# Attention beside feed-forward on one core: norm factors tied to the newest logit, the first tile's end in triple steps, list work held back and spread

## The chip, the cores and the metric

The kernel runs on one core of a Trainium2 chip. Its time is the device time of that core in microseconds (us). Before the change three runs took 1851.42, 1851.66 and 1855.57 us, median 1851.66. The profiled execution spans 1847.4 us.

The engines are named as the profile names them: PE is TensorE (PEld its weight loads), DVE is VectorE, ACT is ScalarE, POOL is GpSimd, SP is SyncE. A letter q behind the name stands for the engine's sequencer, which issues transfers.

## The reference

One graph layer on 4096 nodes with 512 features, then a residual and a norm. Only the part that matters:

```python
hs = layer_norm(x); ht = layer_norm(h_target)          # 4096 x 512 each
q = (ht @ Wq + bq).reshape(T, 8, 64) / 8
k = (hs @ Wk + bk).reshape(S, 8, 64);  v = (hs @ Wv + bv).reshape(S, 8, 64)
logits = jnp.where(adj != 0, einsum('thd,shd->hts', q, k), -1e30)
ctx = einsum('hts,shd->thd', softmax(logits), v)
ht = layer_norm(ht + ctx @ Wo + bo)
y = ht + gelu(ht @ W1) @ W2                            # 512 -> 2048 -> 512
return layernorm(x + y)
```

The adjacency matrix is symmetric and sparse: an edge is drawn with probability 0.00195 per ordered pair, then joined with its mirror image and the diagonal, which makes some 17 neighbours to a node, differing from node to node.

## The kernel before

The kernel works on neighbour lists. It has these streams of work, which one program of Python generators weaves together:

- *Projections*: `x` is normed and projected to keys and values, 32 blocks of 128 rows, and stored to a table `kvd` in HBM (one row per node, 1024 numbers).
- *Lists*: each of 32 tiles of 128 adjacency rows is loaded in four quarters of 512 KB; ScalarE takes their sign, VectorE picks the indices of the edges. Nodes are then sorted by degree in two parts of 16 tiles, and a record per node (degree, norm factors of its target row, neighbour indices) is scattered to HBM. Part one is done before the attention starts, part two beside it.
- *Front* of a target tile: its records say which 128 rows of `h_target` to gather; they are normed (line 990), transposed and multiplied with `Wq` to queries `tq`.
- *Attention*: for up to three neighbour slots at a time the K/V rows are gathered (128 rows of 4 KB a slot), multiplied with the query (line 1209), summed to logits `lg` (1213), exponentiated (1217, 1226), multiplied with the values (1173, 1193) and summed on TensorE (1181).
- *End* of a tile (`finish`): sums, reciprocals, the product with `Wo`, the second norm, and a transpose to `h2T`, which is the input of the feed-forward.
- *Feed-forward* of a group of one or two tiles: `pf` (1316), Gelu (1319), `po` (1325), last norm, scatter to `out`.

A generator's `yield cost` says how long its piece is reckoned to take; the stream with the least total goes next, and `yield None` sleeps until another stream has moved. The instructions are written down in this order, but each engine's program is then arranged at build by the framework from its own reckoning of what is ready when, within the dependencies. So a dependency that is added also moves an instruction in its engine's program.

The parts that the change touches (cuts marked with `# ...`):

```python
def quarter(i, h):                          # load a quarter of adjacency tile i
    if i < NA + FILL:                       # NA = 16, FILL = 5: the first 21 tiles
        a = ring[:, (i * NQ + h) % DEEP, :].bitcast(I32)
    else:
        a = turn_of("wide", wide)           # two buffers in turn
    nc.sync.dma_start(a, adj[i * P:(i + 1) * P, h * QW:(h + 1) * QW])
    return a

def edges(i):
    # ...
    for h in range(NQ):
        n = i * NQ + h
        while len(adjs) < min(n + 2, NT * NQ):
            adjs.append(quarter(*divmod(len(adjs), NQ)))
        a, adjs[n] = adjs[n], None
        sg = turn_of("signs", signs)
        nc.scalar.activation(sg, a, AF.Sign, accum_out=dpart[:, i, h:h + 1])      # L728
        ahead = min(n + DEEP - 1, n + 3 + n // 2)
        while len(adjs) < min(max(n + 3, min(ahead, (NA + FILL) * NQ)), NT * NQ):
            adjs.append(quarter(*divmod(len(adjs), NQ)))
        # ... VectorE: product with positions (L733), maxima of segments (L735)
        yield 2.0
    # ... VectorE: decode, sort, keep the rest of the list (L742 to L759)
    yield 4.0

def source(n, j):                           # keys and values of one block
    # ...
    for half, w in enumerate((wk, wv)):
        # ... four matmuls into pkv
        nc.scalar.copy(kvr[:, half * D:(half + 1) * D], pkv)                       # L931
    r0 = 1 + (g * G + j) * P
    nc.scalar.dma_start(kvd[r0:r0 + P, :], kvr)
    return 7.8

def front(i, idle=0):
    rec = recs[i]
    tq = sp.tile([P, 2 * D], F32, name="tq", bufs=3)
    t = tq[:, :D]
    gather(t, h_target, rec[:, TGT:TGT + 1])
    for _ in range(1 + idle):
        yield
    m = rec[:, RST:RST + 2].bitcast(F32)
    nc.scalar.activation(t, t, AF.Identity, bias=m[:, 1:2], scale=m[:, 0:1])       # L990
    yield
    # ... four transposes (L994), four scalings on ScalarE (L997), two yields,
    # ... four matmuls with Wq (L1003), three yields
    nc.vector.scalar_tensor_tensor(tq[:, :D], pq, HD ** -0.5, bqr, ...)            # L1008
    tqs[i] = tq

def first_fronts():                         # EARLY = 2
    for i in range(EARLY):
        prefetch(i)
    for i in range(EARLY):
        fronts[i] = front(i)
    while fronts:
        go_on()                             # one step of every front
        yield 4.0

def attention():
    tails, pend = [], []                    # tails: the ends of tiles under way
    def advance():
        go_on()
        for t in list(tails):
            if next(t, StopIteration) is StopIteration:
                tails.remove(t)
    # ... per tile, per set of up to three slots:
            lg = sp.tile([P, S, H], F32, name="lg")
            nc.vector.tensor_reduce(lg[:, :n, :], ...)                             # L1213
            # ... exp; advance(); yield; values of the set before; advance(); yield

def weights():                              # the last two quarters of W1 and W2
    for q, pool in enumerate(pools):
        yield 10.0
        load_quarter(pool, q + 2, nc.scalar)

def other_lists():                          # tiles 21 to 31, then the sort of part two
    for cost in ed:
        yield 1.5 * cost
    yield from sort(1)

_weave((projections(), 0), (prepare(), 0), (fill(), 0))
# ...
_weave((att, 0), (chain(feed(g) for g in range(len(GROUPS))), 0), (other_lists(), WAIT),
       (weights(), 0))                      # WAIT = 40
```

`prepare` makes the lists of part one, sorts it and runs `first_fronts`; `fill` makes the lists of five more tiles.

Of the kernel before, what the change touches and what calls it, by code (L numbers as in the profile page):

```python
# [8 lines left out]
F32 = mybir.dt.float32  # L9
# [434 lines left out]
def adj_resnorm_kernel(  # L444
# [88 lines left out]
    with tc.tile_pool(name="keep", bufs=1) as keep:  # L533
# [17 lines left out]
        with ExitStack() as late:  # L551
# [149 lines left out]
            held, moms = [], list(range(NT))  # L701
            mvh = wp.tile([P, NT, 2], F32, name="mvh")

            adjs = []
            DEEP = 8
            FILL = 5

            def quarter(i, h):
                if i < NA + FILL:
                    a = ring[:, (i * NQ + h) % DEEP, :].bitcast(I32)  # L710
                else:
                    a = turn_of("wide", wide)
                nc.sync.dma_start(a, adj[i * P:(i + 1) * P, h * QW:(h + 1) * QW])
                return a

# [47 lines left out]
            def keep_rest():  # L763

                while held:
                    nc.sync.dma_start(*held.pop())
# [97 lines left out]
            def project(order, t=None):  # L864
# [54 lines left out]
                def source(n, j):  # L919
                    g, hT = order[n], state[n][1]  # L920
                    if asked or moms:
                        kvr = sp.tile([P, 2 * D], F32, name="tq", bufs=3)
                    else:

                        kvr = ring[:, 8 + (n * G + j) % 3, :]
                    for half, w in enumerate((wk, wv)):
                        pkv = psi.tile([P, D], F32, name="pq", bufs=3)
                        for kc in range(KC):
                            nc.tensor.matmul(pkv, hT[:, kc, j * P:(j + 1) * P], w[:, kc, :],  # L929
                                             start=kc == 0, stop=kc == KC - 1)  # L930
                        nc.scalar.copy(kvr[:, half * D:(half + 1) * D], pkv)  # L931
                    r0 = 1 + (g * G + j) * P
                    nc.scalar.dma_start(kvd[r0:r0 + P, :], kvr)
                    return 7.8
# [23 lines left out]
                        yield cost  # L958


            recs, tqs, h2Ts, done, ready = {}, {}, {}, set(), []

            def gather(dst, table, idx):
                nc.gpsimd.indirect_dma_start(  # L964
# [21 lines left out]
                gather(t, h_target, rec[:, TGT:TGT + 1])  # L986
                for _ in range(1 + idle):
                    yield
                m = rec[:, RST:RST + 2].bitcast(F32)
                nc.scalar.activation(t, t, AF.Identity, bias=m[:, 1:2], scale=m[:, 0:1])  # L990
                yield
                pt = ps.tile([P, KC, P], F32, name="t", bufs=2)
                for kc in range(KC):
                    nc.tensor.transpose(pt[:, kc, :], t[:, kc * P:(kc + 1) * P], ident)  # L994
                hT = tq[:, D:].rearrange("p (c t) -> p c t", c=KC)
                for kc in range(KC):
                    nc.scalar.activation(hT[:, kc, :], pt[:, kc, :], AF.Identity,  # L997
                                         bias=b1r[:, kc:kc + 1], scale=s1c[:, kc:kc + 1])
                yield
                yield  # L1000
                pq = ps.tile([P, D], F32, name="t", bufs=2)
                for kc in range(KC):
                    nc.tensor.matmul(pq, hT[:, kc, :], wq[:, kc, :], start=kc == 0,  # L1003
                                     stop=kc == KC - 1)
# [141 lines left out]
            def first_fronts():  # L1146

                for i in range(EARLY):
                    prefetch(i)
                for i in range(EARLY):  # L1150
                    fronts[i] = front(i)
                while fronts:
                    go_on()
                    yield 4.0

            def attention():


                tails, pend = [], []

                def advance():
                    go_on()
                    for t in list(tails):
                        if next(t, StopIteration) is StopIteration:
                            tails.remove(t)

                def values(i, j0, n, kv, p, cps, after):

# [29 lines left out]
                for group in GROUPS:  # L1198
# [3 lines left out]
                    for i in group:  # L1202
                        cps = ps.tile([P, KC, P], F32, name="cps", bufs=2)
                        while k < len(SG) and SG[k][0] == i:
                            _, j0, n = SG[k]
                            while i not in tqs:
# [3 lines left out]
                                                    tq[:, :D].unsqueeze(1).to_broadcast([P, n, D]),  # L1210
                                                    ALU.mult)
                            lg = sp.tile([P, S, H], F32, name="lg")
                            nc.vector.tensor_reduce(lg[:, :n, :],  # L1213
                                                    kv[:, :n, :D].rearrange("p j (h d) -> p j h d", h=H),
                                                    AX.X, ALU.add)
# [223 lines left out]
            _weave((att, 0), (chain(feed(g) for g in range(len(GROUPS))), 0), (other_lists(), WAIT),  # L1439
# [36 lines left out]
```

## Time and profile before

| | before |
|---|---|
| time, median of 3 | 1851.66 us |
| span of the profile | 1847.4 us |
| mean granted TensorE clock | 0.964 |
| first multiply of a query with keys (L1209) | 311.25 us |
| first feed-forward matmul (L1316) | 369.81 us |
| last list quarter signed (L728) | 575 us |
| data moved | 463.27 MB |

Until some 290 us the projections and lists run, until about 1705 us attention and feed-forward together, and from there feed-forward alone. The profile's page gives, for each engine, its busy time and the busy share in 40 equal slices. A line of a group or of an order of time reads: line of the kernel, engine, operation, output from inputs, shapes, count; in brackets or behind a bar is the idle time of that engine just before, and what ended it. A wait reads: who waited, for whom, total us, how often, longest.

### The profile page before, as it was taken

The page shows a single profiled execution, that of the slowest core. Times are in us where ns is not written, and L with a number is a line of the kernel's source. Part 1 is how long each engine was busy: PE and PEld are TensorE (multiplying, and loading weights), DVE is VectorE, ACT ScalarE, POOL GpSimd, SP SyncE. Part 2 cuts the span into 40 slices and gives each one's busy share as a digit, 9 for nine tenths or more (in the row PEclk, how much of TensorE's full clock was granted, in tenths as well). Part 3 has the DMA queues.
Part 4 walks back from the last instruction along what each step waited for, and adds up shares of the span by engine and source line. Part 5 has one row for each costly group of instructions (what it writes and reads, how often), then busy time and mean ns, then how long its engine had stood idle before and what let it go on. Part 6 is the DMA issues. An engine that isn't in the chain of part 4 may idle for free. (4 is left out here: it accounts for less than half of the span.)

```text
span 1847.4 us, 22879 instructions
## 1 busy us (share of the span) xinstructions
PE 1693.9 (92%) x7030; PEld 1101.0 (60%) x7030; DVE 1428.8 (77%) x2596; ACT 1222.2 (66%) x3121; POOL 971.7 (53%) x834
## 2 busy tenths in 40 slices
PE   7999884697988989999998998999999999999997
PEld 3444332475655656767676656666666666666664
DVE  6999855999989838686968989979787797988200
ACT  5777634587877646686767867687767676787311
POOL 1000153856546577656567787776574665664001
PEclk9999987898999989999999999999999999999999
DMA  9999949988876738677769878687676767775000
GB/s 350 374 388 374 348 156 350 348 300 303 285 271 209 243 96 313 230 252 260 275 225 315 293 265 295 221 298 253 233 265 216 251 225 247 236 248 170 12 12 25
DMA packets 144396, 463.27 MB, mean 251 GB/s; under 512 B 20628, under 2 KB 25800, under 8 KB 144264
## 3 DMA queue, kind: packets, MB, share of 16 engines
q0 software_dynamic: 96656, 342.64, 54.2%
q1 hardware_dynamic: 39792, 96.00, 14.5%
q10 hardware_dynamic: 7816, 23.08, 3.3%
q8 instruction: 58, 0.95, 0.2%
q14 instruction: 74, 0.61, 0.1%
HBM read 430.76 MB, written 30.89 MB: 250 GB/s over the span
## 5 line engine op out<-in xcount | busy, mean ns | idle before, releaser
L964 POOL DMA_INDIRECT kv<-kvd,rec x603 | 744.9, 1235 | 395.1 <-PE cps L1181 157.2
L1325 PE MATMUL po<-w,gt 128*128 128x512 f32 x1024 | 470.4, 603 | 9.7 <-ACT gt L1319 7.2
L1316 PE MATMUL pf<-h2T,w 128*128 128x256 f32 (+1 forms) x2176 | 466.6, 368 | 1.1 <-issue 0.7
L1316 PEld LDWEIGHTS pf<-h2T,w 128*128 128x128 f32 x2176 | 388.7, 191 | 66.6 <-issue 22.4
L1209 DVE TENSOR_TENSOR kv<-kv,tq 128x1536 f32<-128x1536 f32 (+2 forms) x211 | 352.0, 1676 | 82.4 <-DMA kv<-kvd,rec 71.2
L1193 ACT ACTIVATE kv<-kv,pa 128x64 f32<-128x64 f32 x1520 | 390.8, 336 | 4.1
L1213 DVE TENSOR_REDUCE lg<-kv 128x24 f32<-128x1536 f32 (+2 forms) x211 | 350.2, 1667 | 1.1 <-DVE kv L1209 0.2
L1325 PEld LDWEIGHTS po<-w,gt 128*128 128x128 f32 x1024 | 190.7, 194 | 210.3 <-issue 201.5
L1181 PE MATMUL cps<-ident,kv 128*128 128x128 f32 x2008 | 264.6, 280 | 51.1 <-DMA kv<-kvd,rec 24.2
L1181 PEld LDWEIGHTS cps<-ident,kv 128*128 128x128 f32 x2008 | 238.2, 145 | 120.2 <-DVE kv L1173 51.5
L1173 DVE TENSOR_TENSOR kv<-kv,p 128x1024 f32<-128x1024 f32 (+1 forms) x211 | 251.5, 1194 | 41.2 <-ACT p L1217 28.8
L687 POOL TENSOR_TENSOR n_rs<-n_ve,mhalf 128x2 f32<-128x2 f32 (+2 forms) x51 | 47.7, 936 | 340.8 <-DVE n_ve L680 139.8
L728 ACT ACTIVATE kv<-kv 128x1024 uint8<-128x1024 int32 x128 | 134.7, 1054 | 76.8 <-DMA kv<-in_adj_dram 40.6
L1319 ACT ACT_TABLE_LOAD x104 | 133.4, 1283 | 1.6
L735 DVE MAX8 cand<-kv 128x8 uint16<-128x103 uint16 (+1 forms) x640 | 130.2, 252 | 1.7 <-issue 0.7
L1003 PE MATMUL t<-wq,tq 128*128 128x512 f32 x256 | 119.9, 611 | 12.1 <-ACT tq L997 12.1
L1319 ACT ACTIVATE gt<-pf 128x512 f32<-128x512 f32 x128 | 76.4, 597 | 81.0 <-PE pf L1316 66.7
L929 PE MATMUL pq<-wk,h2T 128*128 128x512 f32 x256 | 121.6, 618 | 5.2 <-ACT tq L931 3.7
L929 PE MATMUL pq<-wv,h2T 128*128 128x512 f32 x256 | 118.5, 606 | 6.7 <-ACT kv L931 5.5
L1107 PE MATMUL t<-wo,rb 128*128 128x512 f32 x256 | 120.7, 614 | 0.0
L990 ACT ACTIVATE tq<-tq,rec 128x512 f32<-128x512 f32 x32 | 26.0, 813 | 142.8 <-DMA tq<-in_L_gnn_h_target_dram,rec 136.3
L1217 ACT ACTIVATE p<-lg 128x24 f32<-128x24 f32 (+2 forms) x179 | 38.9, 218 | 94.6 <-DVE lg L1213 69.3
(156 smaller groups left out, 1603.3 us busy)
## 6 DMA issues: line engine op xcount, KB each, us to landing
kv<-in_adj_dram SPq DMA_DIRECT2D x128, 512.0 KB
kvd<-tq ACTq DMA_DIRECT2D x24, 512.0 KB
kv<-kvd,rec POOLq DMA_INDIRECT x603
kv<-in_L_gnn_h_target_dram SPq DMA_DIRECT2D x32, 256.0 KB
kv<-in_x_dram SPq DMA_DIRECT2D x15, 512.0 KB
rest_d<-gid SPq DMA_DIRECT2D x32, 160.0 KB
w<-in_L_gnn_W_dram SPq DMA_DIRECT2D x4, 1024.0 KB
kvd<-kv ACTq DMA_DIRECT2D x8, 512.0 KB
```

Source lines behind the costliest of these rows:

```text
L728: nc.scalar.activation(sg, a, AF.Sign, accum_out=dpart[:, i, h:h + 1])
L735: nc.vector.max(cand[:, h * SQ + s, :], wd[:, w0:w1])
L929: nc.tensor.matmul(pkv, hT[:, kc, j * P:(j + 1) * P], w[:, kc, :], start=kc == 0, stop=kc == KC - 1)
L964: nc.gpsimd.indirect_dma_start(out=dst, out_offset=None, in_=table[:, :], in_offset=bass.IndirectOffsetOnAxis(ap=idx, axis=0))
L1173: nc.vector.tensor_tensor(v4, v4, p[:, j0:j0 + m, :].unsqueeze(3) .to_broadcast([P, m, H, HD]), ALU.mult)
L1181: nc.tensor.matmul(cps[:, c, :], kv[:, j, D + c * P:D + (c + 1) * P], ident, is_transpose=True, start=j0 + j == 0 and c == 0, stop=j0 + n ...
L1193: nc.scalar.mul(v, v, pa[:, hd:hd + 1])
L1209: nc.vector.tensor_tensor(kv[:, :n, :D], kv[:, :n, :D], tq[:, :D].unsqueeze(1).to_broadcast([P, n, D]), ALU.mult)
L1213: nc.vector.tensor_reduce(lg[:, :n, :], kv[:, :n, :D].rearrange("p j (h d) -> p j h d", h=H), AX.X, ALU.add)
L1316: nc.tensor.matmul(pf[:, k, :], w1[(f0 + k) // KC][:, kc, (f0 + k) % KC * P:((f0 + k) % KC + 1) * P], h2T[:, kc, :w], start=kc == 0, stop= ...
L1319: nc.scalar.activation(gt, pf, AF.Gelu_apprx_tanh)
L1325: nc.tensor.matmul(po[j], gt[:, k, j * P:(j + 1) * P], w2[(f0 + k) // KC][:, (f0 + k) % KC, :], start=False, stop=f0 + k == FC - 1, skip_g ...
```

## The change

Four edits, all about order:

1. *Norm factors tied to the newest logit.* Ahead of a front's norm, VectorE writes the two norm factors over themselves with an operation that also reads the newest logit (`max(m, m)` with the logit as an ignored operand). So the norm can't be placed ahead of that logit. For the first two tiles the operand is a late K/V block of the projections (from the fifteenth pair on), their gathers are asked for at once, and the rest waits until such a block has been written down.
2. *First tile's end in triple steps.* Until the first `h2T` exists, each `advance` takes three steps of a tile's end in place of one.
3. *Lists held.* Once the first fronts are done, the next two quarters of adjacency get a one-column write of the newest logit ahead of their load, so that the load can't be placed ahead of the logits.
4. *Lists spread more widely.* A piece of list work beside the attention is reckoned at 1.8 of its cost in place of 1.5, and `keep_rest` stores what is left before the sort.

The purpose: engines should not stand at a transfer that is not there yet, the first gathers should have the transfer engines to themselves, and the first feed-forward should begin sooner.

```diff
-            adjs = []
+            adjs, held_back = [], []
@@ def quarter
                     a = turn_of("wide", wide)
+                    if fronts_done and len(held_back) < 2:
+                        held_back.append(i)
+                        nc.scalar.copy(a.bitcast(F32)[:, 0:1], latest[-1])
@@ def source
                         nc.scalar.copy(kvr[:, half * D:(half + 1) * D], pkv)
+                    if n >= 14:
+                        latest[:] = [kvr[:, 0:1]]
@@ def front
                 m = rec[:, RST:RST + 2].bitcast(F32)
+                nc.vector.scalar_tensor_tensor(m, m, latest[-1], m, op0=ALU.bypass, op1=ALU.max)
                 nc.scalar.activation(t, t, AF.Identity, bias=m[:, 1:2], scale=m[:, 0:1])
@@ def first_fronts
                     fronts[i] = front(i)
+                    step(fronts, i)
+                while not latest:
+                    yield None
@@ def attention
-                        if next(t, StopIteration) is StopIteration:
-                            tails.remove(t)
+                        for _ in range(1 if h2Ts or begun else 3):
+                            if next(t, StopIteration) is StopIteration:
+                                tails.remove(t)
+                                break
+                    if h2Ts:
+                        begun.add(True)
@@
                             lg = sp.tile([P, S, H], F32, name="lg")
+                            latest[:] = [lg[:, 0, 0:1]]
@@ ahead of the second weave
+            fronts_done.append(True)
             def other_lists():
                 for cost in ed:
-                    yield 1.5 * cost
+                    yield 1.8 * cost
+                keep_rest()
                 yield from sort(1)
```

More of the change, by code (lines that the diff above doesn't have):

```diff
@@ L958, in project @@
                         yield cost
-            recs, tqs, h2Ts, done, ready = {}, {}, {}, set(), []
+            recs, tqs, h2Ts, done, ready, latest = {}, {}, {}, set(), [], []
+            fronts_done = []
             def gather(dst, table, idx):
@@ L1156, in attention @@
             def attention():
-                tails, pend = [], []
+                tails, pend, begun = [], [], set()
                 def advance():
```

## The prediction

> **What bounds the kernel now.** I read the busy times and the slices first. TensorE is the fullest engine, and the slices say where it is not full.
>
> The page of the kernel before, busy times and three rows of its 40 slices (one slice is 46 us):
> ```profile
> PE 1693.9 (92%) x7030; PEld 1101.0 (60%) x7030; DVE 1428.8 (77%) x2596; ACT 1222.2 (66%) x3121; POOL 971.7 (53%) x834
> ...
> PE   7999884697988989999998998999999999999997
> ...
> DVE  6999855999989838686968989979787797988200
> ...
> PEclk9999987898999989999999999999999999999999
> ```
> TensorE lacks 153 us of the span, mostly early. From slice 38 on, VectorE is nearly done and TensorE still runs dense: the end is feed-forward work alone. So the time is TensorE's work plus its holes, and a hole closed anywhere moves the end. Busy time by stage gives TensorE's idle time: 0-262 us 25; 262-275 6; 275-311 16; 311-345 18; 345-370 9; 370-445 11; 445-690 23; 690-1705 33; the rest 5.
>
> Then TensorE's order of time at the change of stage (start, duration, last the idle time before it and what ended it):
> ```profile
> 264.94 3.70 PE L929 MATMUL pq<-wk,h2T 128*128 128x512 f32 x8 [0.61 <-ACT h2T L914]
> 274.16 6.43 PE L929 MATMUL pq<-wv,h2T 128*128 128x512 f32 x8 [5.52 <-ACT kv L931]
> ...
> 319.45 2.82 PE L1181 MATMUL cps<-ident,kv 128*128 128x128 f32 x12 [24.25 <-DMA kv<-kvd,rec]
> ```
> Two holes: one ended by ScalarE's copy out of PSUM, the long one by the first gathered keys and values. What ScalarE did in the first:
> ```profile
> 265.29 1.01 ACT L914 ACTIVATE h2T<-pt,cols 128x256 f32<-128x256 f32 x2
> 272.82 0.81 ACT L990 ACTIVATE tq<-tq,rec 128x512 f32<-128x512 f32 x1 [6.52 <-DMA tq<-in_L_gnn_h_target_dram,rec]
> 273.54 0.56 ACT L931 COPY kv<-pq 128x512 f32<-128x512 f32 x1
> ```
> The norm of the first target tile (L990) stands ahead of the projections' copies in ScalarE's program and waits 6.52 us for its gather, so the copy behind it is late and TensorE stops. The waits say that this repeats, ScalarE's first in the whole run (total us, times, longest):
> ```profile
> ACT tq L990 <- DMA tq<-in_L_gnn_h_target_dram,rec: 136.3, 28, 14.0
> ```
> and three of TensorE's from 230 to 1700 us:
> ```profile
> PE t L1003 <- ACT tq L997: 12.1, 7, 3.8
> PE t L1090 <- ACT h2T L1138: 10.3, 3, 7.1
> PE t L994 <- ACT tq L990: 7.2, 2, 5.8
> ```
> ScalarE waits longest in sum for the gathered target rows. It is not the bound, so most of that costs nothing; what TensorE loses behind the front's steps is in the three lines.
>
> At the same place the list loads (SyncE's queue, order of time):
> ```profile
> 278.52 11.46 SPq L713 DMA_DIRECT2D kv<-in_adj_dram  x4
> 295.19 0.33 SPq L766 DMA_DIRECT2D rest_d<-gid  x1
> 295.61 23.19 SPq L713 DMA_DIRECT2D kv<-in_adj_dram  x6
> ```
> Ten adjacency quarters of 512 KB are asked for between 278 and 319 us, just when the last K/V rows are stored (last issue 290.13), two weight quarters are loaded (262.6 to 290.5) and the first gathers go out (300.81). The DMA share is 0.91 in 275-311 and 1.01 in 311-345.
>
> **What the Trainium skill says.** Perfetto Trace Analysis, Sequencer Loop: an engine's instruction is pushed into its queue and waits there for its semaphores. Read with the trace, what stands behind it waits too: the copy at 273.54 above was held by L990. DMA: Bandwidth & Descriptors, Issuing engines are not separate DMA queues: transfers from ScalarE, SyncE and GpSimd run on the same 16 DMA engines and interleave. The trace agrees: with list loads and weights under way, the first gather, issued at 300.81, served its multiply only at 311.25. TensorE: Matmul & The Clock Gate, What's actually happening: an idle window of about 3.4 us halves TensorE's clock until it has been busy again. The trace agrees: the eight matmuls after the 5.52 us hole took 6.43 us, the same eight 3.60 us at full clock. VectorE: DVE Perf Modes, the section on the TRN2 errata: a small operation has a fixed cost; 128x2 takes 163 ns here (L692).
>
> **The change part by part.**
>
> *Norm tied.* Adds 32 VectorE operations on 128x2, by L692's 163 ns 5.2 us, on an engine that is 77% busy: I count +1. It moves L990 behind the newest logit (for the first two tiles, behind a late copy of the projections). At 266-274 it should take away the hole of 5.52 us and the slow clock after it, 6.43-3.60 = 2.83: **-8**. In 445-690 TensorE's two large holes, 7.10 (ended by L1138 after a 6.72 us wait of L990) and 5.84 (ended by L990 itself), sum to 12.9; half of it, with a little clock, **-7**. In 690-1705 the front's later step (L1003 after L997) accounts for some 11 of 33 idle us; half: **-5**. I take halves because the wait may turn into another in the same queue.
>
> *Lists held.* The list code asks for two quarters ahead, so by the count of loads (43 of 128 from 240 us on, hence number 85, from 0, at 240.25) the two that are held are the first two of the four at 278.52, and the others follow them through the two buffers. All ten loads, 5.2 MB, leave the stretch 278-319. From the last store's issue to the first multiply it is 21.1 us now. Of the ten, the first four and about four of the six fall in it: 4.2 MB, at the 360 GB/s or so that these stretches move about 12 us of DMA time. Not all stood ahead of what the gather needs: half of it, **-6**.
> The work does not vanish. ScalarE has signed 94 quarters by 318 us; with the hold it would be 86, so two tiles of list work move. A tile costs VectorE 9.8 us (the list lines sum to 19.6 us for eight quarters in 395-445). These 20 us were done while VectorE waited for gathers, and now fall where it is 96% busy (72.0 of 75 us in 370-445). The wider spread (1.8 for 1.5) only makes room for them: 81 us of list work over the 230 us to 575, now 103 over 276, 35% against 37%. A third of 20 as a cost: **+6**.
>
> *First tile's end in triple steps.* The first tile's sums come at 334.20, its first feed-forward matmul at 369.81: 35.6 us, of which the operations themselves are some 12 to 15; the rest is waiting between rows of other tiles' work. It could come 12 us sooner. TensorE idles 9 us in 345-370, and the next group's feed-forward (443.53) does not move with it, so part of the gain comes back as a hole ahead of that: **-5**.
>
> Sum: +1-8-7-5-6+6-5 = -24, that is 1851.7-24 = 1828 us, 1.3% less.
>
> **Rivals.** (1) *The norm's wait only changes its name.* ScalarE already waits 69.3 us for logits at L1217, and with the tie L990 waits for VectorE as well. If a query then comes late, VectorE's wait for L1003 (42.6 us in 10 pieces now) grows. For: VectorE is starved at times by gathers (71.2 us). Against: the front has a lead of several steps. Only the transition would gain: 1835 to 1842.
> (2) *VectorE becomes the bound to 690 us.* The deferred lists and full attention share it, and the feed-forward starves. For: 46 busy us of 46 in 414-460. Against: TensorE is dense then most of the time, with 79.5 of 90 us in 370-460. Then +15 on my sum: 1843, in the worst case 1860.
> (3) *The part-two sort comes too late or falls badly.* Its 16 scatters hold the gather queue at 646-676 us, and VectorE idles 6.8, 6.8 and 11.7 us after them. With the lists later they move to some 700 us or more. Their records are wanted only for tiles past the sixteenth; 12 of 32 had been fetched by 688, so I expect no more than a shift. If they are late: +10 to +20.
> (4) *The holes close further than by halves*, since the attention starts some 14 us sooner and every later hole also costs clock: all of the 13, 11 and 12 us gives 1805 to 1812.
>
> **Range and chances.** The sum has two firm terms (8 and 6 at the transition) and softer ones of 5 to 7 that depend on how the instructions fall in each queue. I take 1804 to 1850. Over 2% faster means below 1814.6, which needs rival 4 or most of it: 0.25. Over 2% slower, above 1888.7, would need rivals 2 and 3 together and beyond: 0.04.
>
> **What would show it.** Right: L990's wait for the gather falls from 136 us to under 60; no hole over 2 us in TensorE at 266-274; no adjacency load between some 270 us and the first logit but at most two; the first multiply at 296 to 300 in place of 311.25 and the first feed-forward matmul near 345; TensorE's idle time about 20 us less. Wrong: the idle time of TensorE as long as before but under other names, L1008 or L1217 waiting longer, TensorE thinner in 370-690 than 287 of 320 us, or the first gather still held to 300 us by something other than the lists.

## The result, and the profile after

The changed kernel took 1843.27 us (median of 4 runs, 1841.82 to 1844.49), the kernel before 1853.62 us beside it (4 runs, 1851.42 to 1855.88). The ratio is 0.9944, with a 95% interval of 0.9926 to 0.9962: 0.56% less, where 1.3% less was predicted. The profiled execution spans 1842.8 us, against 1847.4 before. The lines below have numbers of the new file; the norm L990 of before is L1000, the tied operation ahead of it is L999.

The page of the changed kernel, busy times and two rows of its slices (46 us each):
```profile
PE 1695.2 (92%) x7030; PEld 1106.8 (60%) x7030; DVE 1431.5 (78%) x2628; ACT 1216.1 (66%) x3117; POOL 971.5 (53%) x834
...
PE   7999885786989899899999998989999999999997
...
DVE  6999854999988865776888898988887797988200
```
The shape of the bound has not changed. TensorE does the same 7030 matmuls and lacks 147.6 us of the span in place of 153.5. The thin slices 5 to 9 are still thin (8 5 7 8 6, before 8 4 6 9 7). Slices 12, 14 and 21 went from 8 to 9; slices 13, 16 and 26 went from 9 to 8, and slice 16 (737 to 783 us) is one where TensorE was full before.

TensorE's idle time by stage, from the busy times of each engine in stretches (length minus busy, us), shows it with the sign of each piece:

| stage, us | before | after | change |
|---|---|---|---|
| 0-275 | 31.3 | 28.2 | -3.1 |
| 275-345 | 34.3 | 32.6 | -1.7 |
| 345-445 | 19.6 | 22.3 | +2.7 |
| 445-690 | 22.6 | 15.2 | -7.4 |
| 690-850 | 0.0 | 11.0 | +11.0 |
| 850-1240 | 21.5 | 25.1 | +3.6 |
| 1240-1705 | 11.5 | 0.4 | -11.1 |
| 1705 to the end | 12.7 | 12.9 | +0.2 |
| sum | 153.5 | 147.6 | -5.9 |

Two of these entries are one thing, the time round the 16 scatters of the part-two sort. Busy times in 650-690 us (length; busy us and instructions of PE, PEld, DVE, ACT, POOL; granted clock; DMA share; GB/s), first before, then after:
```profile
650.00:690.00 40.00, 32.80 (x146) 22.59 (x145) 15.27 (x14) 15.64 (x42) 28.98 (x27) 0.91 0.33 90
650.00:690.00 40.00, 40.00 (x188) 28.32 (x187) 25.43 (x21) 23.89 (x65) 22.90 (x23) 1.00 0.70 231
```
The dip of 7.2 us that lay here before now lies behind 690 us and has grown to 11.0. In 445-650 hardly anything changed: 15.4 idle us before, 15.2 after. So some 16 us were gained, 11.1 of them in 1240-1705, and 10 given back. The experiments ask which part of the change pays for which.

**The change of stage.** TensorE's order of time (start, duration, last the idle time before and what ended it):
```profile
268.10 3.60 PE L933 MATMUL pq<-wv,h2T 128*128 128x512 f32 x8
279.01 1.97 PE L1004 MATMUL t<-ident,tq 128*128 128x128 f32 x8 [7.32 <-ACT tq L1000]
280.78 5.18 PE L933 MATMUL pq<-wk,h2T 128*128 128x512 f32 x8
```
The first hole is still there: 7.32 us, some 5 us later than the old one of 5.52, and the eight matmuls behind it take 5.18 us for 3.60 at full clock. It is again ended by the norm. What ScalarE did:
```profile
265.81 1.07 ACT L935 COPY kv<-pq 128x512 f32<-128x512 f32 x2
278.15 0.81 ACT L1000 ACTIVATE tq<-tq,rec 128x512 f32<-128x512 f32 x1 [11.26 <-DVE rec L999]
...
279.57 0.56 ACT L935 COPY kv<-pq 128x512 f32<-128x512 f32 x1
```
The norm still stands ahead of a copy of the projections, and now waits 11.26 us, for the tied operation. VectorE says why that was late:
```profile
273.98 0.49 DVE L751 SCALAR_TENSOR_TENSOR gid<-kv,segoff 128x320 f32<-128x320 uint16 x1 [15.45 <-DMA rest_d<-gid]
...
277.89 0.35 DVE L999 SCALAR_TENSOR_TENSOR rec<-rec,kv 128x2 f32<-128x2 f32 x2
```
The tied operation's own data were there, but it stands in VectorE's program behind a list operation (L751) that writes `gid`, and `gid` was still to be read by the store of an earlier list. That store waits in SyncE's program (here the issues of transfers, in order of time):
```profile
240.27 0.33 SPq L717 DMA_DIRECT2D kv<-in_adj_dram  x1
262.87 0.38 SPq L1269 DMA_DIRECT2D degs<-rec  x1
263.34 14.24 SPq L770 DMA_DIRECT2D rest_d<-gid  x2
333.85 0.33 SPq L717 DMA_DIRECT2D kv<-in_adj_dram  x1
```
SyncE issued nothing from 240.3 to 262.9 us: the load of the node degrees `degs`, needed only for a last verdict at the end of the kernel, had been placed there, and it can't go before the sorted records are written. Behind it stood the store of the list, behind the store VectorE's list operation, behind that the tied operation, and behind that ScalarE's norm. Two things wait for the norm: TensorE's transposes of the first tile (L1004), which here stand ahead of the last projections in TensorE's program, and the copy at 279.57 us. The chain runs through the programs of four engines, each in order. The store's data were complete at about 253 us, so the load held it for some 10 us; of VectorE's wait the other 10 are the store itself, issued at 263.34.

The same lines show that the hold worked as a hold: from the list store at 263 to 333.85 us there is no adjacency load. The first gather was issued at 297.58 (300.81 before), and the first multiply came at 305.75 (311.25 before).

**The waits.** ScalarE's longest, whole run (total us, times, longest):
```profile
ACT p L1236 <- DVE lg L1232: 99.5, 58, 6.0
```
and ScalarE's for the norm from 230 to 1700 us:
```profile
ACT tq L1000 <- DMA tq<-in_L_gnn_h_target_dram,rec: 22.2, 4, 9.1
ACT tq L1000 <- DVE rec L999: 12.9, 3, 11.3
```
The wait for gathered target rows fell from 136.3 us to 22.2. The exponentials' wait for logits grew instead (L1217 had 69.3, its line L1236 has 99.5): ScalarE now waits where it has nothing else to do.

**The stretch of the loss.** Busy times in stretches of the changed kernel, in the same form:
```profile
690.00:740.00 50.00, 45.24 (x199) 29.30 (x197) 28.54 (x33) 28.65 (x67) 34.08 (x31) 1.00 0.45 144
740.00:800.00 60.00, 53.77 (x237) 37.38 (x238) 44.34 (x46) 34.80 (x103) 39.77 (x35) 0.94 0.76 258
```
The sort's 16 scatters ran at 702 to 733 us, 55 us later than before (647 to 675). While they hold the gather queue the DMA share falls to 0.45. VectorE waits for gathers afterwards (11.82 us at 737.70, 10.28 at 787.15), and TensorE is idle for 11.0 of the 110 us in 690-800.

### The profile page after: what moved, and what is told of

It is laid out like the page before. It is cut to its first block, busy times and chain, and to the rows that moved or that the text cites. A ratio compares the mean times of both kernels' runs of the same rounds, so it can differ in the third digit from the quotient of the medians.

```text
span 1842.8 us, 22926 instructions
## 1 busy us (share of the span) xinstructions
PE 1695.2 (92%) x7030; PEld 1106.8 (60%) x7030; DVE 1431.5 (78%) x2628; ACT 1216.1 (66%) x3117; POOL 971.5 (53%) x834
## 5 line engine op out<-in xcount | busy, mean ns | idle before, releaser
L1335 PE MATMUL pf<-h2T,w 128*128 128x256 f32 (+1 forms) x2176 | 473.2, 371 | 1.8 <-issue 1.5
L1335 PEld LDWEIGHTS pf<-h2T,w 128*128 128x128 f32 x2176 | 392.6, 193 | 66.3 <-issue 22.1
L1199 PEld LDWEIGHTS cps<-ident,kv 128*128 128x128 f32 x2008 | 242.5, 146 | 120.5 <-issue 57.4
L1199 PE MATMUL cps<-ident,kv 128*128 128x128 f32 x2008 | 267.2, 282 | 49.2 <-DVE kv L1191 34.3
L1191 DVE TENSOR_TENSOR kv<-kv,p 128x1024 f32<-128x1024 f32 (+1 forms) x211 | 251.5, 1193 | 19.9 <-ACT p L1236 19.6
L1236 ACT ACTIVATE p<-lg 128x24 f32<-128x24 f32 (+2 forms) x179 | 39.2, 219 | 129.1 <-DVE lg L1232 99.5
L1117 PE MATMUL t<-wo,rb 128*128 128x512 f32 x256 | 116.1, 596 | 0.0
L933 PEld LDWEIGHTS pq<-wk,h2T 128*128 128x128 f32 x256 | 50.1, 203 | 70.4 <-issue 51.9
```

Of the source, the lines that this page charges most:

```text
L1191: nc.vector.tensor_tensor(v4, v4, p[:, j0:j0 + m, :].unsqueeze(3) .to_broadcast([P, m, H, HD]), ALU.mult)
L1199: nc.tensor.matmul(cps[:, c, :], kv[:, j, D + c * P:D + (c + 1) * P], ident, is_transpose=True, start=j0 + j == 0 and c == 0, stop=j0 + n ...
L1335: nc.tensor.matmul(pf[:, k, :], w1[(f0 + k) // KC][:, kc, (f0 + k) % KC * P:((f0 + k) % KC + 1) * P], h2T[:, kc, :w], start=kc == 0, stop= ...
```

## The experiments

Fifteen kernels, each timed in five rounds against the kernel before on the same chip. Executions of one kernel scatter by up to 1% (before: 1845 to 1865 us in these batches), so I compare ratios to before, with their 95% intervals, and not medians. "Tie", "hold", "spread" and "triple" are the four edits of the change.

| kernel | median, us | ratio to before | interval |
|---|---|---|---|
| all four (the change) | 1843.27 | 0.9944 | 0.9926-0.9962 |
| without tie | 1876.61 | 1.0114 | 1.0090-1.0137 |
| without hold | 1839.37 | 0.9926 | 0.9897-0.9955 |
| without triple | 1851.32 | 0.9973 | 0.9956-0.9989 |
| without spread | 1838.63 | 0.9910 | 0.9879-0.9941 |
| tie alone | 1831.08 | 0.9859 | 0.9827-0.9890 |
| tie + hold | 1836.71 | 0.9904 | 0.9870-0.9939 |
| tie + spread | 1840.71 | 0.9915 | 0.9882-0.9947 |
| tie + triple | 1834.13 | 0.9875 | 0.9847-0.9902 |
| tie + triple, lists later | 1844.83 | 0.9946 | 0.9922-0.9970 |
| all four, lists at once | 1859.53 | 1.0023 | 1.0008-1.0039 |
| all four, first norms on the last block | 1835.20 | 0.9889 | 0.9865-0.9913 |
| A: first norms on the last block, load of degrees late, two more early lists | 1824.46 | 0.9820 | 0.9787-0.9853 |
| A + weights held | 1830.74 | 0.9859 | 0.9827-0.9891 |
| A, lists later, old spread | 1829.52 | 0.9850 | 0.9822-0.9878 |
| A without hold (best) | 1815.82 | 0.9794 | 0.9771-0.9816 |

TensorE's idle time by stage for those that carry the argument, worked out as above from one profiled execution each (busy below it; all have 7030 matmuls, and their busy time differs with the mean granted clock: 1704.8 us at 0.957, 1683.2 at 0.971):

| stage, us | before | all four | without tie | tie alone | tie + triple | best |
|---|---|---|---|---|---|---|
| 0-275 | 31.3 | 28.2 | 30.6 | 27.9 | 27.7 | 26.5 |
| 275-345 | 34.3 | 32.6 | 30.3 | 38.2 | 39.9 | 29.7 |
| 345-445 | 19.6 | 22.3 | 20.8 | 19.8 | 19.3 | 19.7 |
| 445-690 | 22.6 | 15.2 | 21.2 | 19.9 | 14.1 | 14.3 |
| 690-850 | 0.0 | 11.0 | 10.2 | 0.0 | 0.0 | 2.4 |
| 850-1240 | 21.5 | 25.1 | 27.3 | 24.1 | 25.7 | 25.0 |
| 1240-1705 | 11.5 | 0.4 | 22.1 | 2.8 | 1.5 | 0.7 |
| 1705 to the end | 12.7 | 12.9 | 12.9 | 12.7 | 12.8 | 12.7 |
| idle | 153.5 | 147.6 | 175.4 | 145.3 | 140.8 | 130.8 |
| busy | 1693.9 | 1695.2 | 1704.8 | 1690.3 | 1683.5 | 1683.2 |

A caution for reading it: a profiled execution is one of several. That of the kernel before (1849.1 us) is among its shortest, that of tie alone (1837.3 us) the longest of its six, so their difference here, 12 us (8.2 of it idle time), is less than the 26 us of the times. The profiles show less than half of what the tie alone gains.

### The tie, taken out and put in alone

Taken out of the change:
```diff
  m = rec[:, RST:RST + 2].bitcast(F32)
- nc.vector.scalar_tensor_tensor(m, m, latest[-1], m, op0=ALU.bypass, op1=ALU.max)
  nc.scalar.activation(t, t, AF.Identity, bias=m[:, 1:2], scale=m[:, 0:1])
```


> The changed kernel without the tied operation (L999); all else kept. Theory (the tie renames ScalarE's waits and is worth little): the norm waits over 100 us for its gathers again, while the waits for logits fall by nearly as much; TensorE's idle time in 445-690 rises by some 7 us and in 690-1705 falls by some 3; the time is 0 to 5 us above the changed kernel's 1843. Rival (the tie is the main gain): 1850 or more.

Put alone into the kernel before (no hold, no triple steps, spread 1.5):
```diff
+ nc.vector.scalar_tensor_tensor(m, m, latest[-1], m, op0=ALU.bypass, op1=ALU.max)
...
+ if n >= 14:
+     latest[:] = [kvr[:, 0:1]]
...
      fronts[i] = front(i)
+     step(fronts, i)
+ while not latest:
+     yield None
...
+ latest[:] = [lg[:, 0, 0:1]]
```

> The kernel before with the tie alone (the first two tiles' norm on a K/V block from the fifteenth pair on, the others on the newest logit); no hold, no triple steps, spread 1.5. Theory A (the tie is worth some 30 us only because the held and spread lists upset the later stage, which it puts right): within 8 us of the kernel before, 1846 to 1860. Theory B (the tie is a gain by itself, and the rest of the change gives most of it back): 1825 to 1840, the norm's wait for its gather under 40 us.

Measured: 1.0114 without it, 0.9859 with it alone. Alone it gives 1.4%, some 26 us; in the presence of the others its absence costs 1.7%, some 31 us. It is the whole gain of the change, and more than the whole: the rival of the first run and theory B of the second hold. ScalarE's longest wait in the whole run, in the kernel without it (where L999 is the norm itself):
```profile
ACT tq L999 <- DMA tq<-in_L_gnn_h_target_dram,rec: 120.4, 21, 11.9
```
The wait is back. And what TensorE waited for in 850 to 1705 us, this kernel first:
```profile
PE po L1343 <- ACT gt L1337: 9.6, 3, 5.9
PE t L1143 <- ACT h L1134: 7.1, 4, 5.8
PE t L1003 <- ACT tq L999: 5.2, 2, 4.8
PE t L1099 <- ACT rb L1093: 3.9, 1, 3.9
```
then the changed kernel:
```profile
PE t L1144 <- ACT h L1135: 4.4, 2, 4.0
...
PE po L1344 <- ACT gt L1338: 2.2, 2, 2.0
```
Of the seven longest waits of each kernel there, those that ScalarE ends sum to 28.6 us without the tie (the four shown, and 2.8 for the front's later step) and to 11.2 with it (the two shown, and 2.6 and 2.0 for the front's steps). The lines that shrank are not only the front's: Gelu (L1337), the second norm (L1134) and the sums (L1093) share ScalarE's queue with the norm that waits. For the longest of them the chain can be followed, here ScalarE and then TensorE, without the tie:
```profile
1288.64 0.82 ACT L999 ACTIVATE tq<-tq,rec 128x512 f32<-128x512 f32 x1 [11.87 <-DMA tq<-in_L_gnn_h_target_dram,rec]
1291.66 6.35 PE L1343 MATMUL po<-w,gt 128*128 128x512 f32 x8 [5.91 <-ACT gt L1337]
```
The Gelu that TensorE waited for began at 1291.01, behind the norm. In the same way the norm's wait of 10.43 us up to 1154.33 stands ahead of the sums and a hole of 3.88, and its wait of 11.43 up to 1216.49 ahead of a hole of 4.79. These three holes make 14.6 us. The 5.76 ahead of L1143 at 1020.18 are another matter: no norm waits there, and the changed kernel has 4.03 at the same step. So the mechanism is that of the prediction, but wider, and most of it late: in 1240-1705 TensorE is idle for 22.1 us without the tie and 0.4 with it. The smaller holes there I have not traced to the norm. Of the 37 us between the two profiled spans, 27.8 are idle time and 9.6 a longer busy time for the same matmuls (1704.8 for 1695.2), under a mean clock of 0.957 for 0.960.

At the change of stage the tie alone does harm: 275-345 has 38.2 idle us for 34.3. The first gather came at 304.37, the first multiply at 315.71, later than before. Beside the other edits it does nothing there: TensorE's idle time in 0-345 is 60.8 us with the tie and 60.9 without, and the first multiply comes at 305.75 and 305.71.

### Where the first two tiles' norms stand

```diff
- if n >= 14:
+ if n == len(order) - 1 and j == G - 1:
      latest[:] = [kvr[:, 0:1]]
```


> The changed kernel with the first two tiles' norm tied to the last K/V block in place of the fifteenth pair. Theory (the tie failed at the change of stage because the tied operation stands behind list work in VectorE's queue and the norm still ahead of four of ScalarE's copies): TensorE's hole of 7.3 us at 272-279 goes, the projections end some 7 us sooner, the first multiply comes at 298 to 301 in place of 305.75, and the time is 5 to 9 us below 1843. Rival (the transfers hold the first gather at 297 whatever TensorE does): first multiply at 303 to 306, time within 2 us of 1843.

Measured: 0.9889, against 0.9944 for the change; the intervals don't overlap. TensorE's order of time, this kernel:
```profile
277.01 3.60 PE L933 MATMUL pq<-wv,h2T 128*128 128x512 f32 x8
283.71 1.36 PE L1004 MATMUL t<-ident,tq 128*128 128x128 f32 x8 [3.10 <-ACT tq L1000]
```
and ScalarE's:
```profile
282.84 1.52 ACT L1000 ACTIVATE tq<-tq,rec 128x512 f32<-128x512 f32 x2 [5.05 <-DVE rec L999]
284.27 0.56 ACT L935 COPY kv<-pq 128x512 f32<-128x512 f32 x1
```
Tied to the very last block, the norm stands behind all matmuls of the projections, and behind all copies but one: the operand is a column of the block's keys, so the copy of its values (284.27) still comes after the norm, and the last K/V store after that. VectorE waited for the list store no shorter than in the change (17.36 us for 15.45), but the projections no longer stood behind the norm: they ran through at full clock, the last K/V store was issued at 284.86 us (290.05 in the change), and the first multiply came at 297.94, inside the 296 to 300 that the prediction had for the change. So the theory holds, and the 8 us of the prediction exist: the first multiply comes 7.8 us sooner than in the change, and the time is some 10 us less. The change as made didn't take them, because "from the fifteenth pair on" leaves copies of later blocks behind the norm. In the two profiles this gain stands in the busy time (1690.1 us for 1695.2, under a mean clock of 0.969 for 0.960), hardly in the idle time (147.2 for 147.6).

### The hold

Out of the change, and alone beside the tie:
```diff
- if fronts_done and len(held_back) < 2:
+ if False:
```


> The changed kernel without the hold on the two list loads. Theory (VectorE's pace eats the gain: the held list work was done for nothing while VectorE waited, and now fills it up to 445 us): first multiply back at about 311 us, the second group's first feed-forward matmul still at 440 to 446, TensorE's idle time in 370-445 below 15 us in place of 20; the time within 3 us of 1843. Rival (the start of attention sets the rest): second group 5 to 6 us later than 444.6, time 1848 to 1850.

> The kernel before with the tie and the hold; spread 1.5, no triple steps. Theory of the late sort: scatters at 645 to 655 us, time within 4 us of the tie alone (1831), first multiply near 305 against 315.7. Rival (list work moved from idle to full VectorE costs): 5 to 10 us above 1831.

Measured: 0.9926 without it (0.9944 with), and 0.9904 with it (0.9859 for the tie alone). Both differences say that the hold costs, 3 and 8 us, and in both the intervals overlap; a third pair, below, says 5 in the same way. So for the time the theory of the first run holds, and of the second run the rival. The relief of the transfers was larger than predicted: the first multiply comes 9.0 us sooner with the hold than without (305.75, 314.71), and 11.2 beside the tie alone (304.55, 315.71). But the second group's feed-forward begins at 444.58 with it and 445.12 without. Where the early start went is read from VectorE's share of the stretches (the change):
```profile
275.00:311.00 36.00, 17.38 (x41) 8.37 (x42) 11.96 (x29) 10.25 (x26) 13.12 (x14) 0.74 0.70 240
...
370.00:445.00 75.00, 54.75 (x270) 37.42 (x269) 74.81 (x160) 51.83 (x149) 50.49 (x36) 0.86 0.89 326
```
VectorE is idle for 24 of the 36 us in 275-311, when nothing else wants it, and has no idle time left in 370-445. The list lines' share of VectorE, summed by line: with tie alone 18.8 us in 275-345 and 32.8 in 345-445, with the hold beside it 7.2 and 43.2. Ten us of list work went from an engine with time to the same engine without.

### The triple steps

```diff
- for _ in range(1 if h2Ts or begun else 3):
+ for _ in range(1):
```


> The changed kernel without the triple steps. Theory (the first feed-forward comes sooner only to leave a longer hole before the second): first feed-forward matmul 10 to 15 us later than 348.6, hole in 370-445 shorter by as much, time within 3 us of 1843. Rival (the early feed-forward is work gained for good): 8 to 12 us slower, 1851 to 1855.

> The kernel before with the tie and the triple steps; spread 1.5, no hold. Theory: first feed-forward matmul some 20 us sooner than with the tie alone (378.96), total 3 to 6 us below 1831. Rival (it only lengthens the hole before the second group): within 2 us of 1831.

Measured: 0.9973 without them (0.9944 with; the intervals overlap by 0.0006), and 0.9875 with them beside the tie (0.9859 without), a difference lost in the intervals. The first feed-forward matmul comes at 348.62 with them and 378.73 without; the second group's at 444.58 and 453.25. So 30 us at the first tile are 9 at the second and some 5 at the end beside the hold, between the theory's 3 and the rival's 8, and none that can be measured beside the tie alone, where 3 to 6 were expected.

### The spread, and the part-two sort

```diff
- yield 1.8 * cost
+ yield 1.5 * cost
```


> The changed kernel with the spread 1.5 as before. Theory B (the late sort of part two costs the attention its lead): its scatters at some 650 to 690 us in place of 702-733, TensorE's idle time in 690-1705 below 33 in place of 36.5, time 4 to 12 us below 1843. Rival (the spread is needed, VectorE has no room for the lists up to 445): the second group's feed-forward 5 us later than 444.6 and the time 3 to 8 us above 1843.

Put beside the tie alone (1.8 in place of 1.5):

> The kernel before with the tie and the spread 1.8 (and the rest stored ahead of the sort); no hold, no triple steps. Theory (the later sort of part two is what gives the tie's gain back): scatters at about 700 us, TensorE's busy time in 740-840 some 94 us in place of 100, time 6 to 12 us above the tie alone (1831). Rival (the hold does it): within 3 us of 1831.

Measured: 0.9910 without it (0.9944 with), 0.9915 with it beside the tie (0.9859 without). Twice the same sign, 6 and 10 us, both with intervals that overlap, and both times as the theory has them. (The first run leaves `keep_rest` in place; the second brings it in with the 1.8.) What goes with it in the traces is the sort: the first scatter at 644.48 without it, at 701.96 with it; beside the tie 644.16 and 692.30. TensorE's busy time in 690-850 is 159.5 to 160.0 of 160 in the five profiles with the old spread, and 149.0 to 152.0 in the six with the wider one, as long as the lists' start and number are the change's. But with the old spread the dip lies ahead of 690: in 650-850, with both places, TensorE is idle for 5.9 to 7.3 us in the five and for 9.1 to 11.7 in the six.

To move the sort with the old spread, the lists of tie + triple start 40 us later:
```diff
- WAIT = 40.0
+ WAIT = 80.0
```


> The kernel before with the tie and the triple steps and spread 1.5 (ratio 0.9875), its list stream begun at 80 in place of 40. Theory: scatters at 690 to 720, TensorE's busy time in 445-850 380 or less in place of 390.9, ratio 0.991 to 0.995. Rival: 445-850 as before within 3 us, or higher because the second group has VectorE to itself; ratio 0.988 or less.

To leave the wider spread and have the sort early, the lists of the change start at once:
```diff
- WAIT = 40.0
+ WAIT = 0.0
```


> The changed kernel with the list stream begun at 0 in place of 40 of the weave's time, spread 1.8. Theory (the late sort costs): scatters at 650 to 690 us in place of 702-733, TensorE's busy time in 445-850 385 or more in place of 378.8, time 4 to 10 us below the changed kernel (ratio to the kernel before 0.985 to 0.992). Rival (the density of the lists): no change in 445-850, or the second group later than 444.6 and the time the same or longer (ratio 0.994 or more).

The first behaved as the theory of a late sort says: 0.9946 against 0.9875, intervals apart. The busy times in stretches, tie + triple:
```profile
690.00:740.00 50.00, 50.00 (x239) 35.70 (x238) 44.05 (x46) 38.57 (x115) 35.37 (x30) 1.00 0.85 290
740.00:800.00 60.00, 60.00 (x273) 40.51 (x272) 43.87 (x47) 40.79 (x101) 36.94 (x34) 1.00 0.70 240
```
the same with the lists later:
```profile
690.00:740.00 50.00, 47.59 (x212) 31.29 (x210) 28.36 (x33) 31.44 (x77) 32.98 (x31) 1.00 0.44 143
740.00:800.00 60.00, 51.60 (x234) 36.01 (x235) 44.74 (x46) 33.13 (x96) 37.88 (x36) 0.94 0.74 257
```
With the scatters at 637 to 665 us TensorE misses 5.9 us round them (34.1 busy of 40 in 650-690) and nothing in 690-800. With the scatters at 704 to 735 it misses 10.8 (2.4 in 690-740, 8.4 in 740-800) and nothing in 650-690. Between the two places that is a difference of 5 us. Another 9 are missing in 445-650 (187.5 busy of 205 for 196.8), where the later lists now fall, so this kernel doesn't isolate the sort.

The second missed. The sort came early (654 to 682), and the kernel was the slowest but one: 1.0023. The lists then fall beside the first group: TensorE is busy for 106.8 us of 275-445, in the change for 115.2, the first feed-forward comes at 370.39 in spite of the triple steps, and the second group's only at 467.62. Busy time in 445-850 stayed at 379.3 (378.8 in the change), and 690-740 still misses 7.7 us after the earlier scatters (9.8 in 650-850, where the change misses 11.0). So by the one pair of traces a later sort goes with some 5 us more of idle TensorE, and by the other an earlier sort takes only 1 away. That the sort's place is what the spread costs is not shown. In both kernels more is lost beside the tiles where the list work now falls: 9 us in 445-650 and 8.4 in 275-445.

### Towards a better kernel

The chain at the change of stage suggests two more edits on top of the last-block tie: keep the degree load from SyncE's queue by making it wait for the verdict's own data, and let the stream `fill` make two more lists while VectorE is idle before the attention.
```diff
+ nc.vector.tensor_copy(degs[:, i0, :], ok[:, 0:1])
  nc.sync.dma_start(degs[:, i0:i0 + n, :], rec...)
...
- FILL = 5
+ FILL = 7
```


> The changed kernel with three edits: the first two tiles' norm tied to the last K/V block; the small load of degrees for the final verdict made to wait for that verdict, so that it no longer stands in SyncE's queue from 240 us on; seven tiles of lists in place of five before the attention. Theory (two tiles of list work done while VectorE waits take 20 us off it where it is full): transfers busy in 245-262, first multiply at 296 to 300, the second group's first feed-forward matmul at 420 to 430 in place of 438.7, TensorE's idle time in 370-445 below 15 us; time 1815 to 1828. Rival (the loads of the two more tiles push the last K/V stores back): first multiply after 305, time 1833 or more.

To this (A in the table), the last weight quarters held until a logit:
```diff
+ if q >= 2:
+     nc.scalar.copy(w1[q][:, 0, 0:1], latest[-1])
+     nc.scalar.copy(w2[q][:, 0, 0:1], latest[-1])
```


> As the kernel with seven tiles, with the last two quarters of the feed-forward's weights also held to the newest logit, so that they leave ScalarE's queue and the transfer engines until the attention has begun. Theory: ScalarE's wait of 9 us at 254-263 goes and the first multiply comes 4 to 7 us sooner than without; time 3 to 6 us less. Rival: the weights then collide with the first gathers, which fill the transfer engines from 300 to 345 us; no gain, or 3 us more.

To A, the lists 40 us later at the old spread:
```diff
- WAIT = 40.0
+ WAIT = 80.0
...
- yield 1.8 * cost
+ yield 1.5 * cost
```


> The kernel with seven tiles of lists ahead (1824.5), its list stream begun at 80 in place of 40 of the weave's time and spread 1.5, so that fewer lists fall beside the second group. Theory (VectorE's fill sets the second group's start): the second group's first feed-forward matmul 5 to 12 us sooner than 436.35, TensorE's idle time in 370-445 10 to 13 us in place of 18, the sort near 640; time 3 to 8 us less. Rival (the hole moves on, to where the lists now lie): 370-445 fuller, 445-690 emptier by as much, time within 3 us.

From A, the hold taken out (`if False:`, as above):

> The version with seven tiles of lists ahead (ratio 0.982) without the hold. Theory (the hold's early start is eaten by 445): first multiply 5 to 10 us later than 296.9, time within 4 us of that version. Rival (with the lists done ahead the hold keeps its gain): 5 to 9 us slower.

Measured: 0.9820 for A, 0.9859 with the weights held, 0.9850 with the lists later. A's time and its first multiply (296.89) are as its theory has them; its reason is not, for VectorE is still full in 370-445 (75.00 of 75), TensorE's idle time there is 18.2 us where under 15 was expected, and the second group comes at 436.35, not by 430. Neither of the two further edits improved on A, against both theories; their intervals and A's overlap. With the lists later the second group did come sooner (431.19), but 370-445 is emptier (21.3 idle us). Holding the weights only empties the transfers before (DMA share 0.40 in 262-275) and fills them when the attention needs them (1.01 in 311-345); the first multiply fell back to 302.23 and the first feed-forward to 357.88.

Without the hold it is 0.9794 (0.9771 to 0.9816), 1815.82 us, below the kernel before and the change. Against A it is some 5 us less, with intervals that overlap; neither theory nor rival had that, and the first multiply is not later than A's. TensorE's order of time at the change of stage:
```profile
282.13 1.36 PE L1004 MATMUL t<-ident,tq 128*128 128x128 f32 x8 [1.01 <-ACT tq L1000]
```
The hole is 1.01 us. The degrees are loaded at 1681 us and hold nothing of SyncE's back: the list stores go at 241.68 and 254.74 us, seven list loads from 242 to 256, and the next only from 293.70 on, after the first gather (287.97). The two further lists are made early, so the sort comes at 618 to 648 although the spread is 1.8, and 690-850 misses 2.4 us for the change's 11.0. The last K/V store goes at 283.28 and the first multiply comes at 296.44, although the transfers of 275-311 are full (DMA share 1.00). The three edits weren't timed one by one.

## Why the prediction missed

The time, 1843, lies in the predicted range, but the gain is 10.4 us where 24 was predicted. Two steps failed above all: the first tile's -8 was not there, and the spread, counted as nothing, was on the side of the losses. By the prediction's own steps:

- **Norm tied, first tile, -8: failed; measured 0.** TensorE's idle time in 0-345 is 60.8 us in the change and 60.9 without the tied operation; before it was 65.6, with the tie alone 66.1. The step took it that a tie to a late block puts the norm behind the copies. The norm still stood ahead of four of them (279.57 to 289.43), and waited 11.26 us for an operation that was itself held in VectorE's queue, so the hole is 7.32 us for 5.52. The tie to the last block showed what the step had expected. The Trainium skill's Perfetto Trace Analysis, Sequencer Loop, on which the step rested, says that an engine's instruction waits in its queue for its semaphores; I applied it to the norm's queue and not to the queue of the operation that I put ahead of it. The trace agrees with that section in both queues (11.26 us in ScalarE's, 15.45 in VectorE's).
- **Norm tied, 445-690, -7, and 690-1705, -5: the mechanism is real, its places and sizes were wrong.** The two holes that were to be halved, 7.10 and 5.84 us, are still there in the change with 5.73 (at 532.82) and 4.28 (at 595.28). The step passed over a third of 7.20, which ended at 687.13 and belongs to the sort's dip. Ahead of the first the norm now runs at 526.20 without a wait, so what is left of that hole is not the norm's. By pairs of kernels the tie takes 6.0 idle us off 445-690 and 23.1 off 690-1705 beside the other edits, and 2.7 and 6.2 when alone. Of the three chains followed above, 14.6 us, only 4.79 bear the front's name; what waits behind the norm in ScalarE's queue (Gelu, the sums) has other names in the list of waits. The tie as a whole was put at -19 (+1-8-7-5) and measured -26 alone, more than the profiles account for.
- **Hold, -6, and list work into a full VectorE, +6: both terms too small.** The first multiply came 9.0 and 11.2 us sooner by the two pairs, not 6. The cost was taken as a third of 20 us; some ten us of list work moved, and three pairs of runs say a net loss of 3, 8 and 5 us where 0 was predicted, none of which their intervals settle.
- **Spread: counted as nothing.** It is the step that was left out. Rival 3, the late sort, was in the prediction at +10 to +20 and put aside with "I expect no more than a shift". The shift was right (647 to 702 us). TensorE loses 11.0 us in 690-850, against 7.2 at the old place, and the spread costs 6 to 10 us of time by two pairs of runs; that it does so by the sort's place is open.
- **Triple steps, -5:** the first feed-forward came at 348.62 (predicted near 345), worth 5 us beside the hold, as predicted, and not measurable beside the tie alone.
- **Rival 1**, the wait that only changes its name, is half true. ScalarE's wait did rename itself (136.3 to 22.2, and L1217's 69.3 to 99.5), but TensorE kept the gain. **Rival 2**, VectorE the bound to 690, holds in 370-445 alone (74.81 of 75, TensorE 54.75 for 64.47); 370-690 has 284.6 busy us, under the 287 that was named as the sign of it, although the sort's dip of 7.2 has left it. **Rival 4** needed 1805 to 1812; the best kernel, with its different edits, comes near it.
- One reading was off, though no step rests on it: "the rest 5" of TensorE's idle time before is 12.7 us, and the list as it stands sums to 141 of the 153.

Put together: tie -26, and the other three +16 to the measured -10. Hold and spread together cost 0.7% (0.9944 against 0.9875 for tie + triple, intervals apart); which of the two costs how much of it stays open, and so does how much of each small difference is the framework's new order of the programs rather than the edit itself.

## What to carry to other kernels

An operation that ties one engine to another's newest data inherits everything that stands ahead of it in the queue it is put in: before adding it, read what that engine waits for at that moment, and what the one behind that waits for. Size a wait in an in-order engine by all that stands behind it and not by the lines that bear its name, and look for the cause at the far end of the chain (here a small load issued long before it is needed; what moving it is worth by itself was not measured). Work that is held back must have a later place with time to spare on its engine; relief of transfers alone didn't pay.

## What had not been expected

- One load of node degrees, 0.38 us to issue, kept SyncE's queue for 22.6 us (240.27 to 262.87), and through a list store, some 10 us late by it, and VectorE (15.45 us) it reached TensorE.
- The largest gain of the tie lies far from where it was looked for: in 1240-1705 us TensorE's idle time is 22.1 us without it and 0.4 with it (before 11.5, with the tie alone 2.8), at the end of a stretch that the page showed as nearly full.
- In the best kernel the first multiply came at 296.44 us with a DMA share of 1.00 in 275-311, in the change at 305.75 with 0.70 and the list loads held back. The share alone doesn't tell whether a gather is late. In the change without the hold, with a share of 0.83, the gather was issued at 303.94 and the multiply came at 314.71.
